# Messages as three bf16 parts and 32 counted nodes in layers two and three of a relational graph network

## The chip, the cores and the metric

The kernel runs on one core of a Trainium2 chip. The metric is device time in microseconds for one execution. A core has a matrix engine (TensorE, PE in the profile), VectorE (DVE), ScalarE (ACT), GpSimd (POOL), a queue engine (SyncE, SP) that issues transfers, and 16 transfer engines (DMA) that all queues share.

## The reference

N = 6250 nodes with D = 256 features, E = 100000 edges sorted by destination, R = 8 edge types. Destinations are drawn as 6250 u² with u uniform, so low node numbers get very many edges. Three layers of a relational graph network come first:

```python
for l in range(3):
    xr = jnp.einsum('nd,rde->rne', x, W_rel[l])
    msg = xr[edge_type, src]
    agg = jax.ops.segment_sum(msg, dst, num_segments=x.shape[0])
    x = jax.nn.relu(agg + x @ W_root[l] + bias[l])
```

The result is added to the input and layer-normalised (`y`). Then follows an attention step with four heads of 64, in which only the first N edges give an output: `alpha = softmax(leaky_relu(alpha_l[src] + alpha_r[dst]))` over the heads, `tmp[n] = sum_h alpha[n, h] * xt[dst[n], h]`, and a second residual and layer norm. All of it is float32 at the interface.

## The kernel before, in words

*Tiles.* Edges are taken in 782 tiles of 128, nodes in 49 tiles of 128. The kernel sums the source rows first, by destination and type, and multiplies by the weights afterwards: for each node tile, `S[:, r, node]` is the sum of the rows of all sources of type r, transposed, and `dense` (line 577) forms x W_root plus the eight products of S with W_rel in one PSUM tile.

*Hot nodes.* Nodes 0 to 15 (`HOT`) have so many edges that a table is used: `count` (line 640, layer one only) builds `A`, the number of edges of type r from each source to each hot node, by products of bf16 one-hots; `products` (line 670) multiplies A with all rows of x in every layer and adds the sums to S. So the edge tiles that hold only hot nodes are left out of the rest: 36 of them, with 746 left per layer.

*The other edges.* The 746 tiles go in 188 groups of up to four (`GT`), in an order that `Plan.order` fixes: high nodes and low nodes alternate, each kind with a ring of node columns in S of its own (`f` = 0 and 1), and the last six groups are low ones. For a group, `gather` (line 495) has GpSimd issue one indirect transfer per tile: 128 rows of the layer's input, 1024 bytes each, into a message buffer (`msg`, eight buffers of a group). `onehot` (479) has VectorE compare each edge's key, 8 times its place in the tile's window of nodes and its type, with a ramp: f32, 32 to 208 columns. `windows` (504) multiplies messages by one-hots on PE, f32, two products per tile. `add` (521) has VectorE add each window to S at a column that it reads from a table.

*Order.* The scheduler is off: the loop at line 785 writes every engine's instructions in order, once per group, with up to five rounds at the end of a layer for what is left. In a round come, among others: two steps of `count` from round 56 in layer one (`COUNT_AT`), one step of `products` from round 130 (`HOT_AT`), the loads of x rows for node tiles that will be ready, the gathers of the group, the one-hots for the group four ahead, `finish` of node tiles, windows, a few products of `dense`, additions. A node tile is dense once its last group has been added. In layer three two steps of `prepare` (line 710), which makes one-hots for the attention in the memory of A, are in each round from 164 on (`PREP_AT`) that has a low group or comes after the groups.

*Ends.* `finish` (line 598) adds the bias on VectorE, in layers one and two applies relu on ScalarE, and stores 128 rows by SP (lines 606 to 610); `clear` (594) then has ScalarE zero the tile's columns in S. The first gather of the next layer waits for all of these stores. After layer three comes `attention` (line 892).

Of the kernel before, what the change touches and what calls it, by code (L numbers as in the profile page):

```python
# [20 lines left out]
P = 128  # L21
# [4 lines left out]
MARGIN = 800  # L26
HOT = 16
SELS = 6
LOWS = 17
COUNT_AT = 56  # L30
HOT_AT = 130
NEAR = 450
DB = 32
PREP_AT = 164
PIECE = 6
WB = 32
# [7 lines left out]
class Plan:  # L44
# [6 lines left out]

    def __init__(self, N, E, R):
        self.N, self.E = N, E
        self.NT = (N + P - 1) // P
        self.T = (E + P - 1) // P
        self.CH = (self.T + P - 1) // P
        self.W = []
        for c in range(self.CH * P // WB):
            f = min(1.0, (c + 1) * WB * P / E)
            step = 2.0 * N * f / E  # L60
            self.W.append(min(PAD, math.ceil(P * step + 5 * math.sqrt(P) * step + 2)))
        self.WMAX = max(self.W)

        self.TH = 0
        while self.hot_high(self.TH) < HOT - 0.01:
            self.TH += 1
        self.TH -= self.TH % GT


        mid = (self.T + self.TH) // 2  # L70
        self.TM = min(range(mid - 16, mid + 16),
                      key=lambda t: (len(self.shared(t)), abs(t - mid)))

    def reach(self, tiles):
# [43 lines left out]
@with_exitstack  # L118
def kernel(
    ctx: ExitStack,  # L120
    tc: tile.TileContext,
    x: bass.AP,
    src: bass.AP,
    dst: bass.AP,
    edge_type: bass.AP,
    w_rel: bass.AP,
    w_root: bass.AP,
    bias: bass.AP,
    weight: bass.AP,
    attn_l: bass.AP,  # L130
    attn_r: bass.AP,
    out: bass.AP,
):
    nc = tc.nc
    N, D = x.shape
    E = src.shape[0]
    L, R = w_rel.shape[0], w_rel.shape[1]
    H, DH = attn_l.shape
    KC = D // P
    pl = Plan(N, E, R)  # L140
    NT, T, CH, WMAX = pl.NT, pl.T, pl.CH, pl.WMAX
    LAST = N - (NT - 1) * P
    assert R * WMAX * KC <= 512 and E >= NT * P and NT <= P

    const = ctx.enter_context(tc.tile_pool(name="const", bufs=1))
    dram = ctx.enter_context(tc.tile_pool(name="dram", bufs=1, space=DRAM))
    xs = [x] + [dram.tile([N, D], F32, name=f"x{l}") for l in range(1, L)]

    flag = const.tile([1, 1], I32, name="flag")

    fast(tc, const, pl, x, xs, src, dst, edge_type, w_rel, w_root, bias, weight,
         attn_l, attn_r, out, flag)

    bad = nc.values_load(flag[0:1, 0:1], min_val=0, max_val=6 * T)
    with tc.If(bad > 0):
        general(tc, x, src, dst, edge_type, w_rel, w_root, bias, weight, attn_l, attn_r, out)


def fast(tc, const, pl, x, xs, src, dst, edge_type, w_rel, w_root, bias, weight,
         attn_l, attn_r, out, flag):  # L160
# [9 lines left out]
    with ExitStack() as top:  # L170
# [16 lines left out]

        A = tab.tile([P, NT, HOT * R], F32, name="A")

# [12 lines left out]
        with ExitStack() as s:  # L202
            wp = s.enter_context(tc.tile_pool(name="wp", bufs=1))
            sp = s.enter_context(tc.tile_pool(name="sp", bufs=1))
            mp = s.enter_context(tc.tile_pool(name="mp", bufs=8))
            op = s.enter_context(tc.tile_pool(name="op", bufs=AHEAD + 2))
            xp = s.enter_context(tc.tile_pool(name="xp", bufs=3))
            hp = s.enter_context(tc.tile_pool(name="hp", bufs=1))
            ps_w = s.enter_context(tc.tile_pool(name="ps_w", bufs=4, space=PSUM))
# [11 lines left out]
            nc.sync.dma_start(bias_b, bias.rearrange("l d -> (l d)").partition_broadcast(P))  # L221
            fold_weights(tc, mp, w1x, weight, attn_l, attn_r)

# [10 lines left out]

            groups = pl.order()

            ready = {}
            for i, (f, g) in enumerate(groups):
                for j in pl.reach(g):
                    ready[f, j] = i  # L240

            with tc.manual_schedule():
                for l in range(L):
                    wr, wo = load_w(l)
                    opn = layer(
                        tc, pl, l, l == L - 1, groups, ready, S, hold, A, hk, hl, idx, key, pos,
                        iota, ident, wr, wo, bias_b, x, xs, eps, w1x, altab, y,
                        (al3, ga, hif, yT0, lane, dst, iota_p),
                        mp, op, xp, hp, ps_w, ps_d, ps_t, H)

# [211 lines left out]

def layer(tc, pl, l, final, groups, ready, S, hold, A, hk, hl, idx, key, pos, iota, ident, wr, wo,
          bias_b, x, xs, eps, w1x, altab, y, att, mp, op, xp, hp, ps_w, ps_d, ps_t, H):
    nc = tc.nc
# [13 lines left out]
    def onehot(i):  # L479
        g = groups[i][1]  # L480
        w = R * pl.W[g[0] // WB]
        oh = op.tile([P, GT, R * pl.WMAX], F32, name="oh")
        nc.vector.tensor_tensor(  # L483
# [11 lines left out]
    def gather(i):  # L495
        g = groups[i][1]
        msg = mp.tile([P, GT, D], F32, name="msg")
        for q, t in enumerate(g):
            nc.gpsimd.indirect_dma_start(  # L499
                out=msg[:, q, :], out_offset=None, in_=table,  # L500
                in_offset=bass.IndirectOffsetOnAxis(ap=idx[:, t:t + 1], axis=0))
        return msg

    def windows(i, msg, oh):
# [6 lines left out]
        for n, (q, t) in enumerate(reversed(list(enumerate(g)))):  # L511
# [3 lines left out]
            for k in range(KC):  # L515
                nc.tensor.matmul(pw[:, k * w:(k + 1) * w], msg[:, q, k * P:(k + 1) * P],  # L516
                                 oh[:, q, :w], start=True, stop=True)
            res.append((q, t, pw))
# [75 lines left out]
    def clear(f, j):  # L594
        i = nc.scalar.memzero(cols(f, j))  # L595
        tc.add_to_no_dep_group(f"used{l}_{f}_{j}", i.ins)

    def finish(f, j, pd):
        n = rows(j)
# [7 lines left out]
        if not final:  # L607
            h = xp.tile([P, D], F32, name="h", bufs=2)
            nc.scalar.activation(h, pd[:, :D], AF.Relu)  # L609
            nc.sync.dma_start(xs[l + 1][j * P:j * P + n, :], h[:n])  # L610
            return
        z = xp.tile([P, D], F32, name="h", bufs=2)
# [7 lines left out]
        nc.vector.reciprocal(rs, rs)  # L620
        yt = xp.tile([P, D], F32, name="yt", bufs=2)
        nc.vector.tensor_scalar(yt, z, mv[:, 0:1], rs, op0=ALU.subtract, op1=ALU.mult)
# [17 lines left out]
    def count():  # L640

        lows, made, pc = {}, [], None
        pairs = [(n, t) for n in range(HOT) for t in pl.hot_tiles(n)]
        for m in range(len(pairs) + SELS - 2):
# [13 lines left out]
            if m >= SELS - 2:  # L658
# [6 lines left out]
                if t == tiles[-1]:  # L665
                    nc.scalar.copy(A[:, :, n * R:(n + 1) * R],
                                   pc[:, :NT * R].rearrange("p (j r) -> p j r", r=R))
            yield

    def products():  # L670
# [4 lines left out]
        def load(js):  # L675
            t = mp.tile([P, GT, D], F32, name="msg")
            full = len(js) if js[-1] < NT - 1 or LAST == P else len(js) - 1
# [7 lines left out]

        sums = hp.tile([P, D], F32, name="sums")
        for js in loads:
            t = load(js)
            yield
            ph = ps_d.tile([P, 512], F32, name="pd")  # L690
            for n, j in enumerate(js):
                nc.tensor.matmul(ph[:, :D], A[:, j], t[:, n], start=(n == 0), stop=(j == js[-1]))  # L692
            yield
            if js[0] == 0:
                nc.vector.tensor_copy(sums, ph[:, :D])
            else:
                nc.vector.tensor_tensor(sums, sums, ph[:, :D], ALU.add)
        pt = ps_t.tile([P, 4 * P], F32, name="pt")
        for k in range(KC):
            nc.tensor.transpose(pt[:, k * P:(k + 1) * P], sums[:, k * P:(k + 1) * P], ident)  # L700
        for k in range(KC):
            o = cols(1, 0)[:, k * R:(k + 1) * R, :HOT]
            nc.vector.tensor_tensor(
                o, o, pt[:, k * P:k * P + HOT * R].rearrange("p (n r) -> p r n", r=R), ALU.add)
        yield
# [73 lines left out]
    fin, log = [], []  # L779
    counting = count() if l == 0 else iter(())  # L780
    hot = products()
# [3 lines left out]
    for i in range(NG + 5):  # L785

        ahead = i >= PREP_AT and (i >= NG or groups[i][0] == 1)
        if ahead:
            next(prep, None)
        for _ in range(2 if i >= COUNT_AT else 0):  # L790
            next(counting, None)
        if i >= HOT_AT:
            next(hot, None)
# [16 lines left out]
        if i < NG:  # L810
            wins = windows(i, msg, ohs.pop(0))

        n = PIECE * max(1, len(turned)) if i < NG else KC * (R + 1)
# [5 lines left out]
        if i < NG:  # L819
            add(i, wins, vals)  # L820
        if ahead:
            next(prep, None)
        for j in sorted(early.get(i, []), reverse=True):
            xTs[j] = turn(held.pop(j))
        for f, j in sorted((k for k, r in ready.items() if r == i), key=lambda k: -k[1]):
# [4 lines left out]
            turned.append(dense(f, j, None if kept else xTs.pop(j)))  # L830
    assert not (turned or fin or log or held or xTs)
    assert next(counting, None) is None and next(hot, 0) == 0 and next(prep, None) is None
# [42 lines left out]
def halves(A):  # L875

    v = A.rearrange("p j s -> p (j s)").bitcast(BF16)
    n = v.shape[1] // 2
# [499 lines left out]
```

## Time and profile before

| What | us |
|---|---|
| median of 3 runs | 2968.34 (2968.11 to 2978.91) |
| the profiled execution's own time | 2981.72 |
| its span | 2980.0 |
| first to last gather, layer one | 11.32 to 945.38 |
| layer two | 964.78 to 1898.36 |
| layer three | 1919.05 to 2866.81 |
| gathers (POOL, line 499) | 2238 in three layers, 950 ns each |
| window products (PE, line 516) | 1300.7 busy, 8952 records |
| dense products (PE, line 586) | 1130.9 busy, 4800 records |
| window additions (VectorE, line 528) | 904.3 busy |
| one-hots (VectorE, line 483) | 363.9 busy |

An f32 product leaves two records on PE, so 8952 records are 4476 products. A line of an engine's timeline gives the start in microseconds from the span's start, the duration, engine, source line, operation, result and operands, and in brackets the idle time before it with what ended it ("issue": nothing that the profile shows). A line of waits gives the engine and line, what it waited for, the total in microseconds, how often, and the longest. A line of the costliest groups gives the count, busy time, mean of one in nanoseconds, and the idle time before.

### The profile page before, as it was taken

How to read it: one execution, taken by the hardware profiler on the slowest of the kernel's cores; microseconds unless marked ns; L12 is line 12 of the kernel's file. 1: busy time of each engine (PE TensorE's matmuls, PEld its weight loads, DVE VectorE, ACT ScalarE, POOL GpSimd, SP SyncE). 2: the span in 40 equal slices, each digit the busy share in tenths (PEclk: the TensorE clock that was granted, in tenths of full speed). 3: DMA queues.
4: the chain of work that ended last, by engine and by line, in shares of the span. 5: the costliest groups of instructions: out<-in, count | busy, mean ns of one | idle time of the engine just before them, and what ended most of it. 6: DMA issues, size and time to landing. Idle time of an engine off the chain costs nothing.

```text
span 2980.0 us, 45437 instructions
## 1 busy us (share of the span) xinstructions
PE 2684.0 (90%) x15806; PEld 2436.3 (82%) x15807; DVE 1664.3 (56%) x4097; ACT 452.7 (15%) x599; POOL 2136.6 (72%) x2254
## 2 busy tenths in 40 slices
PE   5999999999877899998988987789999999999985
PEld 4998888888776788988877887678888888888874
DVE  7555677764432555555454443355556655554768
ACT  2111111111001011111111010111111111110114
POOL 6777777777775777777777777577777777777731
PEclk9999999999988899999999997799999999998985
DMA  4444444445433444444444544344444444454534
GB/s 151 122 124 123 122 120 123 120 133 159 146 116 106 129 123 122 124 124 117 123 117 148 163 126 117 118 123 127 130 124 128 124 125 128 136 176 137 167 114 167
DMA packets 203054, 388.99 MB, mean 131 GB/s; under 512 B 42885, under 2 KB 128004, under 8 KB 202820
## 3 DMA queue, kind: packets, MB, share of 16 engines
q0 software_dynamic: 107424, 293.48, 34.2%
q1 hardware_dynamic: 92200, 89.76, 9.4%
q8 instruction: 131, 2.15, 0.3%
q10 hardware_dynamic: 3196, 2.76, 0.3%
q14 instruction: 103, 0.84, 0.1%
HBM read 360.18 MB, written 25.65 MB: 129 GB/s over the span
## 4 chain that ended last, share of the span: by engine, by line
PE 70%; POOL 10%; issue 8%; DVE 6%; DMA 3%; ACT 2%; DVEq 0%; ACTq 0%; POOLq 0%; SPq 0%
PE pw L516 31%; PE pd L586 31%; POOL msg L499 10%; PE pd L582 4%; DMA msg<-x,idx 2%; DVE S L528 2%; PE pd L692 1%; PE pt L560 1%; PE pt L636 1%; ACT xT L563 1%; DMA msg<-in_x_dram,idx 1%; PE pd L663 1%; DVE st L1034 0%; DVE z L1022 0%; PE pw L749 0%
## 5 line engine op out<-in xcount | busy, mean ns | idle before, releaser
L499 POOL DMA_INDIRECT msg<-x,idx x1492 | 1417.2, 950 | 504.3 <-issue 420.2
L516 PE MATMUL pw<-oh,msg 128*128 128x160 f32 (+22 forms) x8952 | 1300.7, 302 | 187.4 <-DMA msg<-x,idx 95.2
L528 DVE TENSOR_TENSOR S<-S,pw 128x320 f32 (+22 forms) x2238 | 904.3, 404 | 989.5 <-PE pd L586 504.3
L516 PEld LDWEIGHTS pw<-oh,msg 128*128 128x128 f32 x8952 | 1245.0, 201 | 253.6 <-issue 109.6
L586 PE MATMUL pd<-wr,S 128*128 128x256 f32 x4800 | 1130.9, 386 | 2.2 <-DVE S L528 1.9
L586 PEld LDWEIGHTS pd<-wr,S 128*128 128x128 f32 x4800 | 913.2, 194 | 122.6 <-DVE S L528 3.9
L499 POOL DMA_INDIRECT msg<-in_x_dram,idx x746 | 708.0, 949 | 236.4 <-issue 209.7
L483 DVE TENSOR_TENSOR oh<-iota,key 128x640 f32<-128x640 f32 (+23 forms) x564 | 363.9, 647 | 25.6 <-issue 13.9
L595 ACT ACTIVATE S<-S 128x2048 uint32<-128x2048 uint32 x150 | 285.0, 1900 | 25.9 <-PE pd L586 25.9
L563 ACT COPY xT<-pt 128x256 f32<-128x256 f32 x195 | 72.4, 371 | 1048.1 <-PE pt L560 1046.7
L609 ACT ACTIVATE h<-pd 128x256 f32<-128x256 f32 x98 | 37.7, 385 | 903.3 <-DVE pd L606 669.0
L582 PE MATMUL pd<-wo,xT 128*128 128x256 f32 x588 | 167.8, 411 | 3.2 <-ACT h L609 3.2
L606 DVE TENSOR_TENSOR pd<-pd,bias_b 128x256 f32<-128x256 f32 x147 | 63.2, 430 | 186.6 <-PE pd L586 186.4
L582 PEld LDWEIGHTS pd<-wo,xT 128*128 128x128 f32 x588 | 109.3, 203 | 12.9 <-ACT h L609 3.6
L654 DVE TENSOR_SCALAR sel<-iota,hk 128x392 bf16<-128x392 f32 x138 | 80.4, 613 | 0.0
L619 ACT ACTIVATE rs<-mv,eps 128x1 f32<-128x1 f32 x49 | 14.4, 295 | 403.8 <-DVE mv L618 403.8
L692 PE MATMUL pd<-msg,A 128*128 128x256 f32 x294 | 71.9, 387 | 1.9 <-DMA msg<-x 1.9
L692 PEld LDWEIGHTS pd<-msg,A 128*128 128x128 f32 x294 | 55.6, 196 | 9.1 <-issue 2.2
L560 PE MATMUL pt<-ident,xin 128*128 128x128 f32 x294 | 58.3, 281 | 1.4 <-ACT xT L563 1.4
L636 PEld LDWEIGHTS pt<-w1x,xT 128*128 128x128 f32 x192 | 26.6, 201 | 35.3 <-ACT xT L563 35.3
L560 PEld LDWEIGHTS pt<-ident,xin 128*128 128x128 f32 x294 | 41.8, 147 | 13.2 <-ACT xT L563 2.8
L636 PE MATMUL pt<-w1x,xT 128*128 128x4 f32 x192 | 30.8, 266 | 23.6 <-ACT xT L563 23.6
(187 smaller groups left out, 629.3 us busy)
## 6 DMA issues: line engine op xcount, KB each, us to landing
msg<-x,idx POOLq DMA_INDIRECT x1492, 2.8
x<-h SPq DMA_DIRECT2D x96, 128.0 KB
xin<-x SPq DMA_DIRECT2D x96, 128.0 KB
msg<-x SPq DMA_DIRECT2D x24, 512.0 KB
msg<-in_x_dram,idx POOLq DMA_INDIRECT x746, 2.8
y<-yt SPq DMA_DIRECT2D x49, 128.0 KB
xin<-in_x_dram SPq DMA_DIRECT2D x48, 128.0 KB
msg<-in_x_dram SPq DMA_DIRECT2D x12, 512.0 KB
```

The lines of the kernel that those rows point to most:

```text
L483: nc.vector.tensor_tensor(oh[:, :len(g), :w], iota[:, :w].unsqueeze(1).to_broadcast([P, len(g), w]), key[:, g[0]:g[-1] + 1].unsqueeze(2).t ...
L499: nc.gpsimd.indirect_dma_start(out=msg[:, q, :], out_offset=None, in_=table, in_offset=bass.IndirectOffsetOnAxis(ap=idx[:, t:t + 1], axis=0))
L516: nc.tensor.matmul(pw[:, k * w:(k + 1) * w], msg[:, q, k * P:(k + 1) * P], oh[:, q, :w], start=True, stop=True)
L528: ins = nc.vector.tensor_tensor(o, o, pw.rearrange("p (a b) -> p a b", b=W), ALU.add)
L560: nc.tensor.transpose(pt[:, k * P:(k + 1) * P], t[:, k * P:(k + 1) * P], ident)
L563: nc.scalar.copy(xT.rearrange("p k n -> p (k n)"), pt[:, :D])
L582: nc.tensor.matmul(pd[:, :D], xT[:, k], wo[:, k], start=(k == 0), stop=False)
L586: i = nc.tensor.matmul(pd[:, :D], s[:, k * R + r], wr[:, k, r], start=(xT is None and k == r == 0), stop=(k == KC - 1 and r == R - 1))
L595: i = nc.scalar.memzero(cols(f, j))
L636: nc.tensor.matmul(pt[:, :H], yT[:, k], w1x[:, k, D + H:D + 2 * H], start=(k == 0), stop=(k == KC - 1))
L654: nc.vector.tensor_scalar(oh, iota[:, :NT * R], float(512 * n), hk[:, t:t + 1], op0=ALU.add, op1=ALU.is_equal)
L692: nc.tensor.matmul(ph[:, :D], A[:, j], t[:, n], start=(n == 0), stop=(j == js[-1]))
```

## The change

Layers two and three get their messages from a second table `xb`, of 1536 bytes a row. It holds each value as three bf16 parts that add up to the f32 one: the value rounded, the rest rounded, and what is then left. The one-hots of these layers are bf16, and `windows` forms three bf16 products, summed in PSUM, where one f32 product stood. `finish` makes the parts for the next layer: ScalarE writes the first by a second relu, VectorE the rest in f32, ScalarE the second part, VectorE the third, and SP stores them; the f32 rows are stored as before, and are still used for x W_root.

`A` is bf16 and has columns for 32 nodes in the same number of bytes. Layer one still counts 16 nodes and leaves out 36 tiles; in layer two, `count` runs again from round 8 for nodes 16 to 31 (and for 10 to 15, whose tiles are no longer all covered as before), and layers two and three leave out 52 tiles: 730 tiles, 184 groups. `products` loads the three parts into one buffer of its own and multiplies both halves of A with each of them; in layer one it copies A back to f32 and loads one group ahead. A check that no count is above 256 is added to the flag that selects a general path. The message buffers are eight, seven and six in layers one, two and three; pools for messages, one-hots and tables are opened per layer.

```diff
-HOT = 16
+HOT = 16, 32
-LOWS = 17
-COUNT_AT = 56
-HOT_AT = 130
+LOWS = 15
+COUNT_AT = 46, 8
+HOT_AT = 130, 130
+BUFS = 8, 7, 6
...
+    xb = [None] + [dram.tile([N, 3 * D // 2], F32, name=f"xb{l}") for l in range(1, L)]
...
-        A = tab.tile([P, NT, HOT * R], F32, name="A")
+        A = tab.tile([P, NT, HOT[1] * R], BF16, name="A")
...
+                        mp = u.enter_context(tc.tile_pool(name=f"mp{l}", bufs=BUFS[min(l, len(BUFS) - 1)]))
+                        p = pl if l else first
...
-        oh = op.tile([P, GT, R * pl.WMAX], F32, name="oh")
+        oh = op.tile([P, GT, R * pl.WMAX], BF16 if l else F32, name="oh")
...
-        msg = mp.tile([P, GT, D], F32, name="msg")
+        msg = mp.tile([P, GT, 3 * D // 2 if l else D], F32, name="msg")
         for q, t in enumerate(g):
             nc.gpsimd.indirect_dma_start(
-                out=msg[:, q, :], out_offset=None, in_=table,
+                out=msg[:, q, :], out_offset=None, in_=xb[l] if l else table,
                 in_offset=bass.IndirectOffsetOnAxis(ap=idx[:, t:t + 1], axis=0))
...
-                nc.tensor.matmul(pw[:, k * w:(k + 1) * w], msg[:, q, k * P:(k + 1) * P],
-                                 oh[:, q, :w], start=True, stop=True)
+                if l == 0:
+                    nc.tensor.matmul(pw[:, k * w:(k + 1) * w], msg[:, q, k * P:(k + 1) * P],
+                                     oh[:, q, :w], start=True, stop=True)
+                    continue
+                m3 = msg[:, q].bitcast(BF16)
+                for c in range(3):
+                    nc.tensor.matmul(pw[:, k * w:(k + 1) * w],
+                                     m3[:, c * D + k * P:c * D + (k + 1) * P], oh[:, q, :w],
+                                     start=(c == 0), stop=(c == 2))
...
+    def split(j, pd, t, o):
+
+        r = xp.tile([P, D], F32, name="xres", bufs=2)
+        nc.vector.scalar_tensor_tensor(r, pd[:, :D], 0.0, o[:, 0], op0=ALU.max, op1=ALU.subtract)
+        nc.scalar.copy(o[:, 1], r)
+        yield
+        nc.vector.tensor_tensor(o[:, 2], r, o[:, 1], ALU.subtract)
+        nc.sync.dma_start(xb[l + 1][j * P:j * P + rows(j), :], t[:rows(j)])
...
             nc.sync.dma_start(xs[l + 1][j * P:j * P + n, :], h[:n])
+            t = xp.tile([P, 3 * D // 2], F32, name="yt", bufs=2)
+            o = t.bitcast(BF16).rearrange("p (c d) -> p c d", c=3)
+            nc.scalar.activation(o[:, 0], pd[:, :D], AF.Relu)
+            splits.append(split(j, pd, t, o))
...
+        nodes = range(HOT[0])
+        if l:
+            nodes = [n for n in range(HOT[1])
+                     if n >= HOT[0] or pl.hot_tiles(n) != first.hot_tiles(n)]
...
+                    for c in range(3):
+                        nc.tensor.matmul(ph[:, h * D:(h + 1) * D], A[:, j, h * P:(h + 1) * P],
+                                         part[:, c, n], start=(n == c == 0),
+                                         stop=(j == js[-1] and c == 2))
...
-    counting = count() if l == 0 else iter(())
+    counting = count() if l < 2 else iter(())
...
         if i < NG:
             wins = windows(i, msg, ohs.pop(0))
+        for p in splits:
+            next(p)
...
         if i < NG:
             add(i, wins, vals)
+        for p in splits:
+            next(p, None)
+        splits.clear()
```

## The prediction

> **What bounds the kernel now.** The page comes first, since TensorE's share invites a wrong conclusion:
>
> ```profile
> span 2980.0 us, 45437 instructions
> ...
> PE 2684.0 (90%) x15806; PEld 2436.3 (82%) x15807; DVE 1664.3 (56%) x4097; ACT 452.7 (15%) x599; POOL 2136.6 (72%) x2254
> ```
>
> PE looks like the bound, at 90%, with POOL well behind at 72%. The next view is POOL's timeline, because a share says nothing about how an engine's gaps arise:
>
> ```profile
> 116.03 0.94 POOL L499 DMA_INDIRECT msg<-in_x_dram,idx  x1 [0.30 <-issue]
> 117.28 0.95 POOL L499 DMA_INDIRECT msg<-in_x_dram,idx  x1 [0.30 <-issue]
> 118.53 0.94 POOL L499 DMA_INDIRECT msg<-in_x_dram,idx  x1 [0.30 <-issue]
> ```
>
> Columns are start, duration, operation, and the idle time before it with its cause. Each gather is 0.95 us plus a gap of 0.30 in which POOL waits for nothing: one per 1.2525 us. Of 2238 gathers, 2183 start 1.24 to 1.26 us after the one before. The waits of POOL say how often anything else holds it:
>
> ```profile
> POOL msg L499 <- issue: 629.9, 2066, 0.6
> POOL msg L499 <- PE pw L516: 43.3, 108, 3.5
> POOL msg L499 <- DMA x<-h: 38.2, 2, 19.7
> ```
>
> So POOL never rests inside a layer. In layers one and two, 745 intervals x 1.2525 = 933 us is the whole stretch from first to last gather (11.32 to 945.38 and 964.78 to 1898.36) to within 1 us; in layer three PE holds POOL for 14.6 us more. The 0.30 gaps are counted as idle, which is why 72% hides a full engine. PE is the near second: it follows POOL within the eight message buffers, and what is taken off PE is mostly not taken off the time. The two 19 us waits are the ends of layers one and two, where the next gathers need all rows stored:
>
> ```profile
> 961.26 0.43 DVE L606 TENSOR_TENSOR pd<-pd,bias_b 128x256 f32<-128x256 f32 x1 [7.34 <-PE pd L586]
> ...
> 961.73 0.38 ACT L609 ACTIVATE h<-pd 128x256 f32<-128x256 f32 x1 [7.27 <-DVE pd L606]
> 962.01 1.90 ACT L595 ACTIVATE S<-S 128x2048 uint32<-128x2048 uint32 x1
> 962.14 0.32 SPq L610 DMA_DIRECT2D x<-h  x1
> ...
> 964.78 0.94 POOL L499 DMA_INDIRECT msg<-x,idx  x1 [18.46 <-DMA x<-h]
> ```
>
> Bias, relu, store, and 2.6 us after the store's issue POOL resumes.
>
> **What the Trainium skill says.** "DMA: Bandwidth & Descriptors", section "SWDGE vs HWDGE vs iDMA": for a DMA issued on GpSimd, software computes one read/write descriptor pair per operation, with packets of at most about 4096 B. "Perfetto Trace Analysis", section "DMA Instruction — SWDGE (GPSIMD)": the profiled end is the last descriptor written, not the data's arrival. Together these make a gather's 0.95 us a price per row, not per byte. The trace agrees in part: 1.2525 us holds whether the transfer engines are busy or not, but every gather here has 1024 B rows, so none shows another size. "SBUF — State Buffer", section "SBUF: two separate sides", warns that VectorE in a two-port mode, or reading two SBUF operands, can lock GpSimd out. The 39 ring folds of line 569 read two SBUF operands, and the gathers around all of them keep 1.24 to 1.26 us: no effect here.
>
> **The change, part by part.**
>
> *Gathers (POOL).* Layers two and three lose the 16 edge tiles 36 to 51 that hold nodes 16 to 31: 746 becomes 730 each, 32 x 1.2525 = 40.1 us less on the path. Rows grow from 1024 to 1536 B. Trace price: none. Bounds: nothing below (still 128 rows), proportional to bytes above (0.95 to 1.425, +0.475 each). I take no change, by the two pages.
>
> *Windows (PE).* 1460 f32 products per layer become 4380 bf16 ones. An f32 product leaves two records, 1300.7 / 8952 = 145 ns each, 290 together:
>
> ```profile
> L516 PE MATMUL pw<-oh,msg 128*128 128x160 f32 (+22 forms) x8952 | 1300.7, 302 | 187.4 <-DMA msg<-x,idx 95.2
> ...
> 2784.53 1.18 PE L749 MATMUL pw<-al,A 128*128 128x196 bf16 x12
> ...
> 2907.03 0.21 PE L978 MATMUL p<-v,A 128*128 128x12 bf16 x1
> 2907.09 0.22 PE L974 MATMUL p<-v,A 128*128 128x72 bf16 x1
> 2907.12 0.20 PE L978 MATMUL p<-v,A 128*128 128x12 bf16 x1
> 2907.17 0.22 PE L974 MATMUL p<-v,A 128*128 128x72 bf16 x1
> ```
>
> Twelve bf16 products of 196 columns, each with its own weights, start (1.18 - 0.25) / 11 = 85 ns apart; 72 and 12 columns alternate at 0.08 us a pair, about 43 each. At the mean window of 122 columns I estimate 55 ns; "TensorE: Matmul & The Clock Gate", section "Back-to-back issue gap", gives about 81 at 128 in streams of weight load and product. So 4380 x 55 = 241 us (355 by the page) stands against 1460 x 290 = 423. PE loses 70 to 180 us a layer, nearly all under POOL's 914. Were the gathers free, it would count in full.
>
> *What that does bring.* Layer three's 14.6 us of PE holds: I leave 2, so -12. And the tail: the last windows start at 2885.74, 18.9 us after the last gather at 2866.81; in layer one that lag is 5.6. VectorE, with some 5.1 us of preparation and additions per late group and finishes on top, keeps it near 10: -8. Four fewer groups after group 164 push the last two steps of the attention preparation into the drain: +2. Six buffers instead of eight still let POOL run 30 us ahead.
>
> *Hot products.* 98 records of 244 ns (24 us) become 294 bf16 products of 256 columns, by columns 85 x 256 / 196 = 111 ns: 33 us. +9 a layer, under the PE saving; without it, 9 us on PE. Layer two counts 165 more pairs, 163 ns each on PE (two start 0.49 - 0.33 apart), 27 us, and 613 each on VectorE, 101 us, plus about 30 for low tables and maxima. VectorE has 106 us in 200 there (1060 to 1260) and goes to about 75%: hidden. One-hots stay as they are but for bf16 output. Copying counts to f32 in layer one is 13 ScalarE copies of 0.43 us: hidden.
>
> *Splitting.* Per finished tile: ScalarE relu 0.385 and copy 0.37, VectorE two operations of 0.43, one store of 192 KB on SP. 98 times; 37 us of ScalarE and 42 of VectorE a layer, in their idle time. The new wait: VectorE's first split operation waits for ScalarE's second relu (about 0.9 us), and the last for a copy that ScalarE reaches only after the ring's memzero. Behind it on VectorE stand the next window additions, and PE waits for those to free PSUM; at most 1.4 us a tile. Layers two and three have PE slack for it. Layer one has not: there PE trails POOL by up to 30 of the 40 us that eight buffers allow (group 84, matching windows to gathers along the timelines), so some 22 tiles x 1.4 could cost up to 20 us. I take +2.
>
> *Layer ends.* After the relu at 962.11 now come relu 0.3, memzero 1.9, copy 0.37 and subtraction 0.43, with semaphores, before the last store: +3.3 each. The second drain has shorter windows, -0.6: together +6. The gathers, the next layer's weights and its one-hots all start behind it.
>
> *Transfers.* Gathers take 36.8% of the engines in mid layer two; half as many bytes again makes 55%, and SP's 5.8% about 9: not full. SP's queue also gets 98 stores, and the 786 KB product loads of layers two and three use one buffer; a late one holds PE, not POOL.
>
> Sum: -40 - 12 - 8 + 2 + 2 + 6 = -50. The profiled run took 2981.72 (span 2980.0), so it would become 2932; it lies 13.4 above the median of 2968.34. The gather pace is no less there, so I carry the difference over: 2968 - 50 = 2918.
>
> **The rivals.** *The gather is priced by bytes* (the other side). 1460 gathers get longer, with nothing to hide them: from +34 ns each (50 / 1460, 3.6% of 0.95) the change is no gain, from +45 slower by over 0.5%. In full proportion: 2918 + 1460 x 0.475 = 3612. For it: no size but one in the trace. Against: the two pages.
>
> *The gain is given back in stalls.* POOL stays the pace but is held: the split's waits in layer one (+20), single-buffered product loads (13 a layer, 1 us each, +26 at most). 2918 + 20 + 26 = 2964. For it: PE's 30 us lag in layer one. Against: only 0.9 us of POOL holds there now.
>
> *PE becomes the bound.* If a bf16 product cost what a record costs, 145 ns, windows would be 635 us against 423. PE's 895 a layer would be about 1107, 193 over POOL's 914: 2918 + 386 = 3304. L749's 85 ns at more columns than the mean speaks against it.
>
> *More gain*: the tail and both drains fall to layer one's lag and splits cost nothing: about 2900.
>
> **How the numbers follow.** Forecast 0.68 (own range 2900 to 2945), stalls 0.13 (2940 to 2990), byte price 0.12, more gain 0.04, PE bound 0.03. 2893 to 2975 holds the forecast, the extra gain and three quarters of the stalls: 0.8. Half a per cent, 15 us, is what a measurement of this kernel can tell. Faster (below 2953.5): 0.68 + 0.04 + 0.02 of the stalls = 0.74. Same: 0.08 + 0.01 = 0.09. Slower: 0.17.
>
> **What would show it.** In the changed profile: gathers of layers two and three still 1.25 us apart (above 1.28 the byte price is true); 730 of them from first to last in 914 to 918 us; window products at 45 to 80 ns; POOL's gaps at layer ends 22 to 24 us; last windows within 12 us of the last gather. Wrong if POOL's waits for PE exceed 20 us in any layer, or if PE's chain has no idle time left in layers two and three.

## The result, and the profile after

The forecast was wrong. The kernel after takes 2986.73 us (median of 5, 2981.46 to 2987.64) against 2973.06 for the kernel before (median of 5, 2968.11 to 2978.91): a ratio of 1.0046, interval 1.0028 to 1.0063. That is just inside the half per cent called "the same", 69 us above the forecast and 12 above its range. On another chip, in a run told below, the ratio was 1.0058 (1.0045 to 1.0072). The profiled execution took 2986.66, 4.9 us more than that of before; the one of before was itself 8.7 us above the median of its five runs, and the one of after lies at its median, so the 4.9 us here stand for 13.7 in the medians.

The first view is the top of the page of after:

```profile
span 2984.9 us, 52358 instructions
...
PE 2501.5 (84%) x19163; PEld 2191.6 (73%) x19164; DVE 1840.4 (62%) x4499; ACT 526.1 (18%) x830; POOL 2107.2 (71%) x2222
```

PE has lost 182 us of work, as the change intends, and POOL 29, and the time is not shorter. The gathers say why. This is POOL's timeline in layer two, rows of 1536 bytes:

```profile
1100.87 0.94 POOL L512 DMA_INDIRECT msg<-xb,idx  x1 [0.30 <-issue]
1102.12 0.95 POOL L512 DMA_INDIRECT msg<-xb,idx  x1 [0.31 <-issue]
```

The pace is still one in 1.25 us. What changed is how often POOL is held. The waits of POOL, over the whole execution:

```profile
POOL msg L512 <- issue: 623.4, 1972, 18.4
POOL msg L512 <- PE pw L535: 48.6, 81, 4.7
POOL msg L512 <- PE pw L530: 36.1, 43, 5.2
...
POOL msg L512 <- DMA xb<-yt: 22.6, 1, 22.6
```

Before, PE held POOL in the 0.30 us gaps and for 14.6 us of layer three. Now it holds it for up to 5.2 us at a time: line 535 is the bf16 windows of layers two and three, line 530 the f32 windows of layer one. A count by layer puts a figure on it. I take the stretch from a layer's first gather to its last, less 1.2525 us for each interval, and call the rest its hold:

| us | before: stretch, hold | after: stretch, hold | difference of the stretch |
|---|---|---|---|
| layer one (746 gathers) | 934.1, 0.9 | 963.3, 30.2 | +29.2 |
| end of layer one | 19.4 | 23.55 | +4.15 |
| layer two (746, then 730) | 933.6, 0.5 | 941.2, 28.1 | +7.6 |
| end of layer two | 20.69 | 19.37 | -1.3 |
| layer three (746, then 730) | 947.8, 14.6 | 914.6, 1.6 | -33.1 |
| last gather to the end | 113.2 | 111.6 | -1.6 |

The differences add up to the 4.9 us. Layer three does what was forecast. Layers one and two are held for 58 us, of which the forecast had 2.

What TensorE waited for in layer two of after (975 to 1935 us), in its view of waits:

```profile
PE pd L774 <- DMA x<-xb: 24.3, 7, 8.7
PE pd L705 <- DVE top L710: 21.0, 11, 3.7
PE pd L602 <- DVE xres L623: 13.8, 8, 3.0
```

All three waits are new: before, the work on `pd` waited 0.4 us in this layer. The first, for the loads of the products, comes back below. `pd` is a pool of two PSUM tiles of one bank each (`ps_d`, line 210 before), and three kinds of work take tiles from it in turn: `dense` (602, 606), the counts (705) and the hot products (774). Line 710 is the maximum that the change adds to `count`:

```python
nc.scalar.copy(A[:, :, n * R:(n + 1) * R], pc[:, :NT * R]...)       # 708
nc.vector.tensor_reduce(top[:, n:n + 1], pc[:, :NT * R], AX.X, ALU.max)   # 710, new
```

It reads the PSUM tile, so the tile is not free when ScalarE has copied it, but when VectorE has reached this instruction. Line 623 is the first VectorE operation of a split; it reads the finished tile, which before was free after ScalarE's relu. This is one such case in layer one, from the timeline of all engines:

```profile
625.97 2.05 DVE L548 TENSOR_TENSOR S<-S,pw 128x320 f32 x4 [4.12 <-PE pd L606]
626.13 0.48 ACT L708 CAST A<-pd 128x392 bf16<-128x392 f32 x1 [9.71 <-PE pd L705]
...
627.93 0.62 DVE L696 TENSOR_SCALAR sel<-iota,hk 128x392 bf16<-128x392 f32 x1
...
628.47 0.55 DVE L710 TENSOR_REDUCE top<-pd 128x1 f32<-128x392 f32 x1
...
629.08 0.49 PE L705 MATMUL pd<-sel,low 128*128 128x392 bf16 x1 [2.98 <-DVE top L710]
...
629.36 3.52 PE L530 MATMUL pw<-oh,msg 128*128 128x64 f32 x16
...
633.14 0.94 POOL L512 DMA_INDIRECT msg<-in_x_dram,idx  x1 [2.77 <-PE pw L530]
```

ScalarE is done with the tile at 626.61. VectorE comes to the maximum after four window additions, which themselves waited for PE, and a one-hot, and ends it at 629.02. PE, in order, stands for 2.98 us before the next node's first count product, with the window products behind it. Those then run slowly: 16 records of them (8 f32 products) took 3.52 us, where the same form took 1.89 to 2.00 us in the neighbouring rounds. The message buffer is free that much later, and POOL stands for 2.77 us. From the end of the copy to the end of the maximum, the 38 counted nodes average 1.6 us (up to 4.3), where 0.6 is the operation itself.

The Trainium skill's page "TensorE: Matmul & The Clock Gate", section "What's actually happening", says that PE's clock falls to half after an idle window of about 3.4 us and comes back after as long a busy one. The granted clock here shows the half (0.51 from 629 to 633 us), though the pause was shorter, 2.98 us; from 652 to 657 us it is back at 0.90. In the next view, of busy times by stretch, columns are the stretch, its length, busy time and count of PE, PEld, DVE, ACT and POOL, then PE's granted clock (1.00 is full speed), DMA share and GB/s:

```profile
629.00:633.00 4.00, 3.92 (x18) 3.85 (x18) 0.98 (x4) 0.00 (x0) 1.07 (x2) 0.51 0.25 75
647.00:652.00 5.00, 4.76 (x20) 4.67 (x21) 2.82 (x10) 0.00 (x0) 2.17 (x3) 0.50 0.35 104
```

The second stretch follows one more new wait. The check that no count is above 256 ends in a product of its own (line 718), for which PE waits 3.80 us behind VectorE; the window products after it run at half clock, and a gather is held behind them:

```profile
647.24 0.19 PE L718 MATMUL pt<-most 128*1 128x1 f32 x2 [3.80 <-DVE most L716]
...
652.05 0.95 POOL L512 DMA_INDIRECT msg<-in_x_dram,idx  x1 [2.27 <-PE pw L530]
```

Longer stretches show the same in the mean. Before, in layer one:

```profile
330.00:460.00 130.00, 125.53 (x748) 111.52 (x749) 92.70 (x207) 21.84 (x27) 98.31 (x105) 1.00 0.42 121
...
620.00:720.00 100.00, 93.42 (x578) 85.03 (x577) 51.02 (x124) 14.69 (x20) 75.67 (x80) 0.98 0.50 149
```

and after:

```profile
330.00:460.00 130.00, 118.99 (x691) 105.38 (x690) 94.65 (x208) 23.57 (x39) 90.78 (x96) 0.97 0.42 123
...
620.00:720.00 100.00, 89.92 (x534) 81.67 (x533) 54.82 (x135) 17.76 (x30) 61.91 (x66) 0.93 0.40 118
```

PE is less busy, slower, and POOL makes 9 and 14 gathers fewer.

### The profile page after: what moved, and what is told of

Read it like the earlier page. It is cut to its first block, busy times and chain, and to the rows that moved or that the text cites. A ratio compares the mean times of both kernels' runs of the same rounds, so it can differ in the third digit from the quotient of the medians.

```text
span 2984.9 us, 52358 instructions
## 1 busy us (share of the span) xinstructions
PE 2501.5 (84%) x19163; PEld 2191.6 (73%) x19164; DVE 1840.4 (62%) x4499; ACT 526.1 (18%) x830; POOL 2107.2 (71%) x2222
## 5 line engine op out<-in xcount | busy, mean ns | idle before, releaser
L512 POOL DMA_INDIRECT msg<-xb,idx x1460 | 1386.9, 950 | 511.8 <-issue 415.9
L606 PE MATMUL pd<-wr,S 128*128 128x256 f32 x4800 | 1137.1, 387 | 22.5 <-DVE S L548 19.4
L535 PE MATMUL pw<-oh,msg 128*128 128x192 bf16 (+19 forms) x8760 | 587.4, 225 | 201.5 <-DMA msg<-xb,idx 146.1
L535 PEld LDWEIGHTS <-msg 128*128 128x128 bf16 x8760 | 536.5, 102 | 291.3 <-DMA msg<-xb,idx 139.8
L530 PEld LDWEIGHTS pw<-oh,msg 128*128 128x128 f32 x2984 | 413.6, 201 | 95.0 <-issue 42.0
L530 PE MATMUL pw<-oh,msg 128*128 128x160 f32 (+22 forms) x2984 | 432.4, 301 | 60.1 <-DVE S L548 24.8
L496 DVE TENSOR_TENSOR oh<-iota,key 128x448 bf16<-128x448 f32 (+40 forms) x556 | 361.1, 651 | 24.4 <-issue 17.3
L696 DVE TENSOR_SCALAR sel<-iota,hk 128x392 bf16<-128x392 f32 x303 | 177.1, 613 | 0.0
L774 PE MATMUL pd<-x,A 128*128 128x256 bf16 x588 | 74.9, 288 | 39.3 <-DMA x<-xb 39.3
L705 PE MATMUL pd<-sel,low 128*128 128x392 bf16 x303 | 78.3, 333 | 28.3 <-DVE top L710 27.9
L774 PEld LDWEIGHTS <-A 128*128 128x128 bf16 x588 | 59.7, 103 | 52.0 <-DMA x<-xb 30.3
```

The lines of the kernel that those rows point to most:

```text
L496: nc.vector.tensor_tensor(oh[:, :len(g), :w], iota[:, :w].unsqueeze(1).to_broadcast([P, len(g), w]), key[:, g[0]:g[-1] + 1].unsqueeze(2).t ...
L512: nc.gpsimd.indirect_dma_start(out=msg[:, q, :], out_offset=None, in_=xb[l] if l else table, in_offset=bass.IndirectOffsetOnAxis(ap=idx[:, ...
L535: nc.tensor.matmul(pw[:, k * w:(k + 1) * w], m3[:, c * D + k * P:c * D + (k + 1) * P], oh[:, q, :w], start=(c == 0), stop=(c == 2))
L606: i = nc.tensor.matmul(pd[:, :D], s[:, k * R + r], wr[:, k, r], start=(xT is None and k == r == 0), stop=(k == KC - 1 and r == R - 1))
L696: nc.vector.tensor_scalar(oh, iota[:, :NT * R], float(512 * n), hk[:, t:t + 1], op0=ALU.add, op1=ALU.is_equal)
L705: nc.tensor.matmul(pc[:, :NT * R], lows[t], oh, start=(t == tiles[0]), stop=(t == tiles[-1]))
```

## The experiments

Theory 1: late readers of the two PSUM banks hold PE, and PE holds the gathers; first the maximum, then the split. Theory 2: counting, now with splits, is too much work for VectorE beside the additions. Two more suspects are the earlier start of counting (round 46 instead of 56) and layer one's product loads, made one ahead, which take a second message buffer.

**Eight runs on chips that could not answer.** The first four kernels, and the next four, came to two chips on which every kernel takes some 3630 us, the kernel before too. The first four (before 3639.79 on their chip):

> The maximum of each counted node is read from the table A in SBUF instead of from PSUM; same work on VectorE, but the PSUM bank is free as soon as ScalarE has copied it. Theory 1 (the bank held until VectorE reaches the maximum makes PE wait in order): POOL's holds above 1.2525 us a gather fall from 30 to about 12 us in layer one and from 28 to about 6 in layer two; time about 2950. Theory 2 (the counting is simply too much work for VectorE while the splits run): holds stay near 30 and 28, time near 2985. Theory 3 (layer one's look-ahead loads take a message buffer): layer one's holds stay above 15.

```diff
-  nc.vector.tensor_reduce(top[:, n:n + 1], pc[:, :NT * R], AX.X, ALU.max)
+  nc.vector.tensor_reduce(top[:, n:n + 1], A[:, :, n * R:(n + 1) * R], AX.XY, ALU.max)
...
```

With this edit, here and in every kernel below that reads the table, the limit of the check goes from 256.5 to 255.5.

> Layer one counts from round 56 as before, nothing else changes. If the early start is what brings the lag to the buffers' limit: layer one's holds fall from 30 us to under 10, layer two's stay at 28; time about 2963. Theory 1: the waits behind the maximum remain wherever counting is put, so layer one's holds stay above 18.

```diff
-COUNT_AT = 46, 8
+COUNT_AT = 56, 8
```

> Layer one's products load a group of rows one step ahead no more, so one message buffer fewer is taken from the gathers from round 130 on. Theory 3: the holds after 640 us (about 18 of layer one's 30) go, layer two keeps its 28; time about 2967. Theory 1: the lag that counting built up is there anyway, holds of layer one fall by less than 8; time 2978 or more.

```diff
-        rows_of, ph, m = {} if l else {0: load(loads[0])}, None, 0
-        yield
+        rows_of, ph, m = {}, None, 0
...
-                if m + 1 < len(loads):
-                    rows_of[m + 1] = load(loads[m + 1])
-                t = rows_of.pop(m)
+                t = load(js)
```

> Layer two counts nothing (the columns of nodes 10 to 31 are left at what layer one wrote or zero, so those sums are left out; A is zeroed on POOL at the start). Theories 1 and 2 both expect layer two's holds to fall from 28 to under 4, and layer one's to stay near 30; time about 2958. If instead the splits or the wider transfers cause layer two's holds, they stay above 15.

```diff
+            nc.gpsimd.memset(A[:, :, HOT[0] * R:], 0.0)
...
-            nodes = [n for n in range(HOT[1])
-                     if n >= HOT[0] or pl.hot_tiles(n) != first.hot_tiles(n)]
+            nodes = []
```

Ratios to the kernel before, in this order: 0.9978 (0.9956 to 1.0001), 1.0018 (0.9998 to 1.0037), 1.0032 (1.0006 to 1.0057), 0.9974 (0.9959 to 0.9988). The timeline of PE in the first of them shows what is different there:

```profile
112.11 0.48 PE L606 MATMUL pd<-wr,S 128*128 128x256 f32 x1 [0.29 <-issue]
112.82 0.48 PE L606 MATMUL pd<-wr,S 128*128 128x256 f32 x1 [0.23 <-issue]
114.22 0.38 PE L606 MATMUL pd<-wr,S 128*128 128x256 f32 x1 [0.92 <-issue]
```

Dense products of one tile, with operands long there, stop between single instructions. In after, the same stretch is an unbroken run. The gathers that are free still follow at 1.25 us, but POOL is held for 200 to 245 us in every layer. Over the whole of e1, POOL waits 396 us for PE's windows and 277 us for a releaser that the profile does not name; 28 us of anything else are hard to find in that. What causes the stutter, and whether it is all of the difference, is not known. The next four (before 3629.67) met the same trouble:

> The maximum of each node's counts is read from the table of counts instead of the PSUM bank; the work is otherwise that of the kernel after. Theory 1 (the bank held by the maximum stops TensorE, and so the gathers): the gathers are held 5 to 15 us in layer one instead of 30 and 4 to 12 in layer two instead of 28, and the time falls by 25 to 40 us against the kernel after, to about 2950. Theory 2 (the counting is too much work for VectorE beside the splits): nothing changes but a few us, the holds stay at 25 to 30 in both layers, time 2980 to 2990.

> Counting in the first layer starts at group 56, where the kernel before starts it, instead of 46. If it is the early start that matters in layer one (counting over before the backlog of the groups has been worked off), the hold of layer one falls from 30 us to under 10 and the time by about 20, layers two and three being as they were. Theory 1: the same bank waits come ten groups later; the hold stays at 20 to 30 us and the time within 10 us of the kernel after.

> No counts in layer two: the table keeps zeros for nodes 16 to 31, and nodes 10 to 15 keep their counts of the first layer, so layer three leaves messages out of its sums; its work is the same. Theories 1 and 2 both: the hold of layer two falls from 28 to under 5 us, layer one stays at 30, time about 2960. If layer two's hold comes from TensorE's own bfloat16 windows or from its single load buffer of products, it stays over 15 us and the time over 2975.

> Four edits at once: each node's maximum is read from the table when the next node's counts are done, counting in layer one starts at group 56, layer one's loads for its products are taken when they are used and not one ahead, and the second part of a split is made from the activation already in SBUF instead of the PSUM bank. Theory 1: the holds of layers one and two fall to 10 us or less each, time 2930 to 2945, below both kernels. Theory 2: they stay near 20 each, time 2965 to 2985.

Ratios 0.9992 (0.9963 to 1.002), 1.0018 (0.9997 to 1.0039), 0.9993 (0.9971 to 1.0014), 0.9999 (0.9972 to 1.0027). The kernel after was not timed on these chips. On the first, e1 and e4 lie 0.4 to 0.6% below e2 and e3, the way in which theory 1 and the cost of counting point; on the second, the four intervals overlap. No size follows from these eight.

**All edits at once.** The remaining runs but the last came to chips on which the kernel before takes about 2970 us. Up to e15 each kernel was executed once, so differences of some 10 us between these times are not to be read: the six runs of one kernel further down span 7 and 12 us. Of the combined kernel's four edits, two were shown above (e2, e3), and two, the late maximum and the split from SBUF, follow in e10 and e13.

> The combined kernel of before once more, for its trace: maxima read from the table one node late, layer one's counting from group 56, layer one's loads not one ahead, the second part of a split made from the activation in SBUF. On a chip [...] (kernel before near 2970 us): theory 1 has the gathers held 10 us or less each in layers one and two and a time of 2930 to 2945; theory 2 has them held near 20 us each and 2965 to 2985. On a chip where the kernel before takes 3640 us: within 0.5% of the kernel before, as the last time, and the run tells nothing of the holds.

2955.35 us beside 2973.81 for the kernel before; holds of 15.9, 8.5 and 1.6 us in the three layers. That is closer to theory 1, but short of its 10 us in layer one and of its 2945.

**One edit each.** First the maximum:

> One of the four edits of the combined kernel alone: each node's maximum is read from the table when the next node's counts are done; the PSUM bank is free once ScalarE has copied it. Theory 1 (the maximum holds the bank and with it TensorE): the holds fall from 30 to 12 to 20 us in layer one and from 28 to about 10 in layer two, the time to about 2955 to 2965. If the other three edits make the combined kernel's gain, the holds stay within 5 us of 30 and 28 and the time near 2985.

```diff
...
+                    if seen:
+                        u = seen.pop()
-                    nc.vector.tensor_reduce(top[:, n:n + 1], pc[:, :NT * R], AX.X, ALU.max)
+                        nc.vector.tensor_reduce(top[:, u:u + 1], A[:, :, u * R:(u + 1) * R],
+                                                AX.XY, ALU.max)
+                    seen.append(n)
...
+        u = seen.pop()
+        nc.vector.tensor_reduce(top[:, u:u + 1], A[:, :, u * R:(u + 1) * R], AX.XY, ALU.max)
...
```

2962.65 us (before beside it 2969.32). Layer one's hold falls from 30.2 to 12.0 us, layer two's only from 28.1 to 21.3, where about 10 was expected. The stretches of layer one that were shown above, in this kernel:

```profile
330.00:460.00 130.00, 121.78 (x718) 107.52 (x718) 97.97 (x216) 25.71 (x43) 95.66 (x102) 0.99 0.43 126
...
620.00:720.00 100.00, 93.58 (x586) 86.04 (x584) 58.24 (x147) 18.88 (x32) 71.30 (x76) 0.98 0.50 149
```

Six and ten gathers are back, and PE's clock with them. In layer two its waits are

```profile
PE pd L602 <- DVE xres L623: 21.8, 10, 3.0
...
PE pd L705 <- ACT A L708: 6.0, 10, 0.7
```

The 21.0 us for the maximum have become 6.0 for ScalarE's copy, but the wait for the split's reader has grown from 13.8 to 21.8: the two share the pair of banks, and part of what one no longer holds the other does.

> Another of the four alone: counting in layer one starts at group 56 instead of 46, all else as after. If the early start is layer one's trouble, its hold falls from 30 us to under 12, layer two stays at 28, time about 2965. Theory 1: the bank waits only come later; layer one's hold stays at 20 to 30 us and the time within 10 us of the kernel after.

2980.41 us; holds 25.0 and 27.9. The early start is at most 5 us of layer one, no more than the hold of one kernel differs between chips (below): the stalls before 600 us shrink, and those at 663 to 704 grow, where counting now ends beside the hot products.

> A third alone: layer one's loads for its products are made when they are used, so that they take one message buffer instead of two. If the second buffer is layer one's trouble, its hold falls from 30 us to under 20, above all after 680 us, layer two stays at 28, time about 2970. Theory 1: the stalls before 660 us stay (15 us or more of them), and the hold is 22 us or more; where the products' TensorE work now waits for its loads, it is not less at all.

2993.01 us; holds 29.9 and 33.2. The second message buffer is not the trouble. The edit also drops an empty step at the start of `products` in layers two and three, so that these begin a round earlier there.

**What else holds layer two.** The split alone, both together, and layer two without counts:

> The second part of a split is made from the activation in SBUF; the maximum still reads the PSUM bank. If late readers of the two banks are the cause (theory 1), this alone gives a part in both layers: the hold falls to 20 to 26 us in layer one and to 14 to 22 in layer two, time 2965 to 2975. If the load on VectorE is the cause, which this edit doesn't change, the holds stay within 4 us of 30 and 28, time near 2985.

```diff
-    def split(j, pd, t, o):
+    def split(j, h, t, o):
...
-        nc.vector.scalar_tensor_tensor(r, pd[:, :D], 0.0, o[:, 0], op0=ALU.max, op1=ALU.subtract)
+        nc.vector.tensor_tensor(r, h, o[:, 0], ALU.subtract)
...
-            splits.append(split(j, pd, t, o))
+            splits.append(split(j, h, t, o))
```

> Both late readers are gone: the maximum from the table one node late, the split's second part from SBUF; counting starts at group 46 and loads go one ahead, as in the kernel after. Theory 1: holds of 12 us or less in layer one and 10 or less in layer two, time 2940 to 2952, below the combined kernel's 2955, as its late load is left out. If load or the other edits made the combined kernel's gain in layer two, the hold there stays at 18 us or more and the time above 2958.

The edits of e10 and e13 together, and nothing else.

> The kernel after without counts in layer two: the table keeps zeros for nodes 16 to 31 and layer one's counts for nodes 10 to 15, so layer three's sums lack messages; its work is the same. Both theories have the hold of layer two fall from 28 us; how far tells what the counting costs in all, its maxima, its loads of VectorE and its TensorE work: under 5 us if the counting is the whole of it, 8 to 15 us if the split's hold of the bank counts without it too. Layer one stays at 30, time 2958 to 2970.

| us | time | hold, layer one | layer two | layer three |
|---|---|---|---|---|
| after | 2986.66 | 30.2 | 28.1 | 1.6 |
| e10, maximum late | 2962.65 | 12.0 | 21.3 | 1.5 |
| e13, split from SBUF | 2974.67 | 27.0 | 21.0 | 0.0 |
| e14, both | 2951.61 | 15.3 | 7.2 | 1.2 |
| e15, no counts in layer two | 2959.13 | 30.2 | 1.5 | 0.0 |

In layer two each edit alone gives 7 us and both give 21 (14 in the timed runs below, so it is open whether both give more than their sum). Layer one stays above what was expected in e13 (20 to 26) and in e14 (12 or less). TensorE's waits in layer two show the remainder changing hands. With the split alone from SBUF:

```profile
PE pd L705 <- DVE top L710: 21.0, 11, 3.7
...
PE pd L602 <- ACT yt L644: 11.2, 9, 2.5
```

and with both:

```profile
PE pd L602 <- ACT yt L644: 17.2, 10, 2.5
...
PE pd L705 <- ACT A L708: 6.0, 10, 0.7
```

Waits on `pd` for its readers sum to 34.8 us in after (21.0 + 13.8), 30.3 in e10 (with two small lines for the split's reader, 1.3 and 1.2), 32.2 in e13 and 23.9 in e14 (with one of 0.7); the hold goes 28.1, 21.3, 21.0, 7.2. The order agrees, but the hold falls by more than the waits do, 7.1 against 2.6 us in e13; what makes the rest is not shown. What is left waits for ScalarE's second relu (line 644), which still reads the bank. That e15 leaves 1.5 us says that the splits and their reader cost next to nothing in layer two without counting. It keeps the wider transfers, the bf16 windows and the single load buffer of the products (23.7 us of TensorE's waits for loads), so none of these holds the layer by itself. It can't say by what counting does its harm, since it takes away its maxima and its load on VectorE together. The share that stays with both readers gone, 7 us here and 13.5 in the next run, is what theory 2 can still claim.

**Timed, on one chip.**

> Both late readers of PSUM banks gone, timed in rounds beside the kernel before. Theory 1: 2945 to 2955 us and a ratio of 0.990 to 0.994 to the kernel before. If the single execution was a lucky one: 2960 to 2985 and a ratio of 0.996 to 1.004. On a chip [...] (kernel before 3630 to 3640 us): a ratio within 0.997 to 1.001, which tells nothing.

> The kernel after, unchanged, on the same chip. 2980 to 2988 us and a ratio of 1.003 to 1.006 to the kernel before; holds of 30, 28 and 2 us in the three layers. The freed version is then 1.0 to 1.3% below it by theory 1. On a chip [...]: 3625 to 3655.

| | median us (6 runs) | ratio to before | holds in the profiled execution |
|---|---|---|---|
| both readers gone | 2950.85 (2949.14 to 2961.24) | 0.9935 (0.9922 to 0.9949) | 19.4, 13.5, 2.6 |
| after, unchanged | 2988.30 (2984.25 to 2991.58) | 1.0058 (1.0045 to 1.0072) | 32.0, 27.8, 1.3 |

The kernel before took 2969.40 (11 runs). So taking both readers away saves 37.5 us, 1.25%, and the change is then 0.65% faster than the kernel before. That is 19 us of the 50 forecast; the readers are the larger part of what was missing, not all of it. The holds of the same kernel on two chips differ by up to 6 us (15.3 and 7.2 against 19.4 and 13.5; the profiled execution here was the slowest of its six), so smaller differences above are not to be read.

**Left open.**

> Both late readers gone and counting in layer one from group 56. If the earlier start of counting holds layer one beside the readers, its hold falls from 15 us to 8 to 11, the stalls at 379 to 505 us being gone, and the time to about 2945. If it only moves the stalls to where counting now ends, beside the products, as it did with the readers in place, the hold stays at 13 to 20 us and the time at 2948 to 2958.

3635.53 us beside 3653.29 for the kernel before: again a chip with a stuttering TensorE, and no answer. Layer one's last 15 to 19 us of hold are unexplained. The check's own product is a candidate: in e10, e14 and e16 TensorE still waits 4.2 us for it in layer one, and its granted clock is 0.51 in the 5 us from 632 on in e14. The copies of A back to f32 are another. No run leaves out either. It was also not separated whether the maximum does its harm only by the bank or also by VectorE's own wait for the copy (15.1 us in after), since the late maximum removes both; the edit that would tell, e1, ran on stuttering chips only.

## Why the prediction was wrong

- **Gathers, -40.1: right.** With 1536-byte rows they take 950 ns and follow at 1.250 us (median). Half as many bytes again changed nothing, as the prediction took from two pages of the skill; the byte rival (3612) is out.
- **Window products: right.** Line 535 has 587.4 us in 8760 records, 67 ns each, in a forecast span of 45 to 80; 294 us a layer, against 241 estimated and 355 by the page's figure.
- **Layer three, -12: right.** Its hold went from 14.6 to 1.6 us and the stretch is 914.6, as forecast.
- **Layer ends, +6: half.** The chain from the bias to the next gather grew as worked out. These are its lines after layer one:

```profile
991.45 0.43 DVE L637 TENSOR_TENSOR pd<-pd,bias_b 128x256 f32<-128x256 f32 x1 [6.08 <-PE pd L606]
...
992.51 1.91 ACT L615 ACTIVATE S<-S 128x2048 uint32<-128x2048 uint32 x1
...
994.31 0.40 ACT L624 CAST yt<-xres 128x256 bf16<-128x256 f32 x1
994.75 0.43 DVE L626 TENSOR_TENSOR yt<-xres,yt 128x256 bf16<-128x256 f32 x1 [1.67 <-ACT yt L624]
995.20 0.32 SPq L627 DMA_DIRECT2D xb<-yt  x1
...
998.13 0.95 POOL L512 DMA_INDIRECT msg<-xb,idx  x1 [22.60 <-DMA xb<-yt]
```

  From bias to gather it is 6.68 us against 3.52, +3.2, with the second part waiting behind the ring's memzero. The whole gaps changed by +4.15 and -1.3, +2.85 in all.
- **Tail, -8 + 2: a quarter of it.** The last windows start 9.0 us after the last gather (2882.34 against 2873.31), as forecast, but their additions start only at 2887.72, behind preparation and a finished tile on VectorE. 1.6 us is what came.
- **Layer two's counting, "hidden": the step that failed.** The load was right: 144.46 us of VectorE in the 200 from 1060 on, 72% against "about 75%". But the maxima were priced only as part of "about 30" us of VectorE time. An operation that reads a PSUM tile has a second price, the time until its engine gets to it, during which PE cannot have the bank. For the split, too, the prediction had a wait of PE, but for the window additions and with "PE slack for it" in this layer, not for the bank. Layer two came to +27.6 us where 0 was forecast; without both readers 14 (timed) to 21 of them go, and what holds the rest is open.
- **Layer one, +2: the same step, missed.** The prediction named its danger, PE 30 us behind POOL of the 40 that the buffers allow, and put only the split's wait there. Splitting alone did nothing at first: up to round 48 the lag of the additions behind the gathers is within 3 us of before (29.9 against 27), and from 54 on, with counting, it is about 10 us more (40.9 against 32 at round 60). The maximum was the larger part: e10 took away 18 of the 29 us, while e13's 3 are too few to be read. TensorE's waits for it in layer one are only 8.2 us; the halved clock after such pauses, shown above, adds to them, but no run measures its share by itself.

The sum: -50 forecast, +4.9 in the profiled executions, a difference of 55; 27 of it from layer one, 28 from layer two, +4 from the tail, -3 from the layer ends, -1 from layer three. The other 14 of the 69 us are the 13.4 that the prediction carried over from a profiled execution above its median: after's lies at its median. The rival with this sign, the gain given back in stalls, had the right end (2940 to 2990) and a chance of 0.13, in part by luck: its mechanisms were the split's wait and single-buffered product loads. The latter do hold PE (39.3 us in the whole execution) but not POOL: layer three has them, and a hold of 1.6 us, and so has layer two of e15, with 1.5. The prediction's own sign of failure, POOL's waits for PE above 20 us in a layer, is what happened.

## What to carry to other kernels

Price a new operation that reads PSUM twice: its time on its engine, and the time until that in-order engine reaches it, in which TensorE can't write the bank; then ask what stands behind TensorE's next user of that pool. Take a check or a second result from the copy in SBUF rather than from the bank, and free all late readers of a shared pool together, since one alone hands part of its wait to the next (13.8 us became 21.8 here). A near-second engine with little slack turns such waits into lost time even where its total work has just been cut.

## What the runs showed of the hardware

- An indirect gather of 128 rows takes 0.95 us and a gap of 0.30 on POOL with 1024-byte and with 1536-byte rows.
- In unbroken runs of 24 bf16 window products, each with its own weights, the starts are 49 ns apart at 112 columns, 56 at 128 and 82.5 at 192 (medians of 11 to 16 runs in after). The skill's "TensorE: Matmul & The Clock Gate", section "Back-to-back issue gap", gives about 81 at 128 columns for such streams; its isolated formula, N / 2.4 + 2.5, gives 49, 56 and 82.5 and is the nearer one here.
- After pauses of 2.98 and 3.80 us TensorE's granted clock was 0.51 and 0.50 for the next 4 and 5 us.
- On three of the chips every kernel took 22% longer than the kernel before took on the others, with TensorE pausing between instructions that waited for nothing in the profile: weight loads of line 535 idle 412 us for "issue" in e1, against 123 in after. There e1 to e8 all lay within 0.4% of the kernel before.
